# A graph network's first layer: the steps that end a block of 128 nodes moved one pair of edge blocks apart, and the two sort instructions put in separate steps

## The chip, the cores and the metric

The kernel runs on one core of one Trainium2 chip. The metric is the device time of one execution in microseconds. TensorE (PE in the profile) does matrix products and transposes, VectorE (DVE) elementwise work and reductions, ScalarE (ACT) activations and copies, GpSimd (POOL) issues the gathers here, and SyncE (SP) issues most other DMA transfers. [...]

## The reference

Four blocks follow each other on a table x of 6250 nodes by 256 values: a graph layer, a mixture of experts whose gates come from an attention over a second graph, a second graph layer, a second mixture of experts. The change touches the first graph layer. What it computes:

```python
xn = layernorm(x)
row, col = edge_index                       # 106250 edges, sorted by col
h = concatenate([xn[row], edge_attr], axis=1)
h = relu(h @ W1 + b1)                       # 106250 x 256
agg = segment_sum(h, col, num_segments=6250)
cnt = segment_sum(ones, col)
agg = agg / maximum(cnt, 1.0)[:, None]
x = x + relu(concatenate([xn, agg], axis=1) @ W2 + b2)
```

The second block begins with `layernorm(x) @ W_gat` and two dot products per node for the attention; the kernel works these out at the end of each block of 128 nodes of the first layer. Its 131072 edges are sorted by the kernel itself.

## The kernel before

Nodes are kept in 49 blocks of 128, called w in the code. A first stage normalises x and computes the node half of both products: `xn @ W1[0:256] + b1` goes to DRAM (`y_dram`), `xn @ W2[0:256]` stays in SBUF (`b_all`). Then comes the main loop of the layer. For each node block there is a window of 18 x 128 sorted edges, in three groups of six; two blocks of 128 edges are a pair, so a node block takes nine pairs, and the loop runs over 441 pairs k.

What happens to a pair:

- `turn` (line 1367): TensorE transposes the pair's edge attributes (tiles `pt<-ident,ea`, line 1072), ScalarE copies them to SBUF (`et<-pt`, line 1073). It runs three pairs ahead. PSUM holds two such transposed pairs, SBUF four copies.
- `hidden` (line 1382): eight passes of TensorE multiply them by W1 (`ph<-w1b,et`, line 1078), VectorE adds the gathered node half (`yg<-ph,yg`, line 1392), ScalarE applies the ReLU (`h<-yg`, line 1397). It runs one pair ahead. PSUM holds three results `ph`.
- `add_up` (line 1399): once in three pairs, a 0/1 matrix (`eq`, built by VectorE at lines 1163 and 1173) times h adds the group's edges into the node block's sum (`pe<-h,eq`, lines 1410 and 1416). There is one such sum in PSUM.
- `load_sources` (line 1357): once in three pairs GpSimd issues six gathers from `y_dram` (`yg<-y_dram,src`, line 1091) into one of three buffers, and `load_attr` has SyncE load the edge attributes of a later group (line 1290).

Beside the pairs run generators, each advanced by one step per pair: a step is what stands between two `yield`. `end_of(w)` starts one pair after the last group of node block w was added up, and its steps are:

1. VectorE divides the sum by the count (`rc`, `o<-pe,rc`, lines 1425 to 1428) and adds b2 to `b_all` (line 1429).
2. TensorE transposes the quotient (`pt<-ident,o`), ScalarE copies it (`gt<-pt`).
3. TensorE multiplies by the second half of W2 (`pt<-w2b,gt`); VectorE adds, applies the ReLU into x (`o<-pt,b_all`, `x_all`, lines 1437 and 1438) and normalises the new x (lines 1049 to 1062, with one square root on ScalarE, line 1053), which ends in `ln_x`.
4. TensorE transposes `ln_x` (`pt<-ident,ln_x`), ScalarE copies it into `b_all`.
5. TensorE multiplies by W_gat (`pt<-wg,b_all`), ScalarE copies (`hb<-pt`, line 1452), VectorE makes the attention terms (lines 1455 to 1459).
6. After each seventh node block a DMA on ScalarE's queue writes `gat_dram`, from which the next block of the network gathers.

The four TensorE steps share one PSUM pool with two buffers. `background` prepares the next windows (counts at line 969, loads, index arithmetic) and sorts the edges of the second graph: 106 times the eight largest of 1024 keys in each partition (`V.max`, line 1225) and their removal (`V.match_replace`, line 1227).

The program is not laid down in the order of the source. A list scheduler gives each engine its order, with the source order as priority, so that an instruction whose inputs are there can be taken forward. The sort, which depends on nothing in the layer, is taken far forward: it fills VectorE's order up to pair 124 of 441.

Of the kernel before, what the change touches and what calls it, by code (L numbers as in the profile page):

```python
# [841 lines left out]
def kernel(ctx: ExitStack, tc: tile.TileContext, a: dict, out: bass.AP):  # L842
# [62 lines left out]
    with ExitStack() as fast:  # L905
# [60 lines left out]
        def count_below(w):  # L966

            if w:
                V.tensor_scalar(
                    junk, flat, float(w * P), None, op0=OP.is_lt, op1=OP.add,  # L970
                    accum_out=below[:, w : w + 1],
                )

        def count_good():

            V.tensor_scalar(
                junk, flat, N - 0.5, None, op0=OP.is_lt, op1=OP.add,
                accum_out=good[:, NB : NB + 1],
            )
            V.tensor_scalar(  # L980
                junk, flat, -0.5, None, op0=OP.is_lt, op1=OP.add,
                accum_out=good[:, NB + 1 : NB + 2],
            )
            V.tensor_sub(
                good[:, NB : NB + 1], good[:, NB : NB + 1], good[:, NB + 1 : NB + 2]
            )

        def find_starts(pool, b):

            sl = slice(b * TB, (b + 1) * TB)  # L990
            tot = pool.tile([P, D], F32, name="pt")
            TE.matmul(tot[:, 0:TB], ones, below[:, sl], start=True, stop=True)
            V.tensor_scalar(start[:, sl], tot[:, 0:TB], float(E1 - WE), None, op0=OP.min)
# [46 lines left out]
        def nodes(table):  # L1040
            return table[0:NP, :].rearrange("(t p) d -> p t d", p=P)
# [15 lines left out]
        def layer_norm(pool, t0, n):  # L1057

            mv, rs = norm_scale(pool, t0, n)
            xn = pool.tile([P, n, D], F32, name="ln_x", bufs=1)  # L1060
            for i in range(n):
                V.tensor_scalar(
                    xn[:, i, :], x_all[:, t0 + i, :], mv[:, i, 0:1], rs[:, i : i + 1],
                    op0=OP.subtract, op1=OP.mult,
                )
            return xn

        def transposed(psum, dst, src, n=2):

            pt = psum.tile([P, n, P], F32, name="pt")  # L1070
            for c in range(n):
                TE.transpose(pt[:, c, :], src[:, c * P : (c + 1) * P], ident)  # L1072
            SC.activation(dst, pt.rearrange("p c k -> p (c k)"), AF.Copy)  # L1073

        def mm(dst, lhs, rhs, n=2):

            for c in range(n):
                TE.matmul(dst, lhs(c), rhs(c), start=c == 0, stop=c == n - 1)  # L1078
# [140 lines left out]
            )  # L1219
            V.tensor_tensor(key.bitcast(I32)[:, half], raw[0], raw[1], op=OP.bitwise_or)  # L1220

        def sort_step(k):

            top = order[:, k * 8 : (k + 1) * 8]
            V.max(out=top, in_=key)  # L1225
            if k * 8 + 8 < KT:
                V.match_replace(out=key, in_to_replace=top, in_values=key, imm_value=0.0)  # L1227

        def sorted_edges(pst, wk):

            k = order.bitcast(I32)
            V.tensor_scalar(src2, k[:, 0:KA], 8191, None, op0=OP.bitwise_and)
            some = key[:, 0:KT]
            for v, s in ((high, 20), (low, 13)):
                vi = some.bitcast(I32)
                V.tensor_scalar(
                    vi, k, s, 127, op0=OP.logical_shift_right, op1=OP.bitwise_and
                )
                V.tensor_copy(some, vi)
                V.tensor_scalar(some, some, -1.0, 127.0, op0=OP.mult, op1=OP.add)  # L1240
                V.tensor_copy(v, some)
            for c in range(KA // P):
                pt = pst.tile([P, 4, P], F32, name="pt")
                TE.transpose(pt[:, 0, :], some[:, c * P : (c + 1) * P], ident)
                lt = wk.tile([P, P], BF16, name="lt")
                SC.activation(lt, pt[:, 0, :], AF.Copy)
                SC.dma_start(low_dram[c * P : (c + 1) * P, :], lt)
            V.tensor_add(good2[:, 1:2], good3[:, 0, 0:1], good3[:, 1, 0:1])
            V.tensor_add(good2[:, 3:4], good3[:, 0, 1:2], good3[:, 1, 1:2])

            lim = key[:, 0:KA]
            for g in range(KA // G):
                V.memset(lim[:, g * G : (g + 1) * G], float(first_block(g)))
            V.tensor_sub(lim, high[:, 0:KA], lim)
            hit = order[:, 0:KA]
            V.tensor_scalar(hit, lim, 0.0, None, op0=OP.is_ge)
            V.scalar_tensor_tensor(hit, lim, NK - 0.5, hit, op0=OP.is_lt, op1=OP.mult)
            V.tensor_reduce(good2[:, 0:1], hit, axis=AX.X, op=OP.add)
# [5 lines left out]
        with ExitStack() as layer:  # L1264
# [77 lines left out]
            with (  # L1342
# [78 lines left out]
                def end_of(w):  # L1421

                    pe = sums.pop(w)
                    rc = wk.tile([P, 1], F32, name="rc")
                    V.tensor_scalar(rc, pe[:, D:WS], 1.0, None, op0=OP.max)
                    V.reciprocal(rc, rc)
                    ag = wk.tile([P, D], F32, name="o")
                    V.tensor_scalar(ag, pe[:, 0:D], rc, None, op0=OP.mult)
                    V.tensor_add(b_all[:, w, :], b_all[:, w, :], b2)
                    yield  # L1430
                    gt = wk.tile([P, D], F32, name="gt", bufs=1)
                    transposed(psm, gt, ag)
                    yield
                    pm = psm.tile([P, D], F32, name="pt")
                    mm(pm, lambda c: gt[:, c * P : (c + 1) * P], lambda c: w2b[:, c, :])
                    o = wk.tile([P, D], F32, name="o")
                    V.tensor_add(o, pm, b_all[:, w, :])
                    V.scalar_tensor_tensor(
                        x_all[:, w, :], o, 0.0, x_all[:, w, :], op0=OP.max, op1=OP.add
                    )  # L1440
                    xn = layer_norm(wk, w, 1)
                    yield
                    yield
                    transposed(psm, b_all[:, w, :], xn[:, 0, :])
                    yield
                    pg = psm.tile([P, D], F32, name="pt")
                    mm(
                        pg[:, 0:HX], lambda c: b_all[:, w, c * P : (c + 1) * P],
                        lambda c: wg[:, c, :],
                    )  # L1450
                    hb = wk.tile([P, HX], F32, name="hb")
                    SC.activation(hb, pg[:, 0:HX], AF.Copy)
                    pa = wk.tile([P, HX], F32, name="pa")
                    for v, dst in ((att_s, gtab[:, w, HX + H :]), (att_d, a_dst[:, w, :])):
                        V.tensor_mul(pa, hb, v)
                        V.tensor_reduce(
                            dst, pa.rearrange("p (h x) -> p h x", h=H), axis=AX.X, op=OP.add
                        )
                    V.tensor_copy(
                        gtab[:, w, 0:HX].rearrange("p (x h) -> p x h", h=H),  # L1460
                        hb.rearrange("p (h x) -> p x h", h=H),
                    )
                    if w % TB == TB - 1:
                        yield
                        sl = slice(w - TB + 1, w + 1)
                        SC.dma_start(nodes(gat_dram)[:, sl, :], gtab[:, sl, :])

                def background():

                    for b in range(1, NB):  # L1470
                        for w in range(b * TB, (b + 1) * TB):
                            count_below(w)
                            yield
                        find_starts(psm, b)
                        yield
                        load_windows(b)
                        yield
                        if b == 1:
                            count_good()
                            yield  # L1480
                        for k in range((b - 1) * 18, min(b * 18, KT // 8)):
                            sort_step(k)
                            yield
                            yield
                    sorted_edges(psm, wk)

                work = [background()]
                load_sources(0)
                for k in range(3):
# [502 lines left out]
        with (  # L1992
# [253 lines left out]
            k, w, done = 0, 0, 0  # L2246
# [24 lines left out]
        with (  # L2271
# [11 lines left out]
            for i in range(2):  # L2283
                k = NB + 1 + 2 * i
# [52 lines left out]
```

## Time and profile before

| What | us |
|---|---|
| Median of three runs (lowest, highest) | 4402.47 (4393.04, 4404.77) |
| The profiled execution, device time | 4419.4 |
| Its span in the profile | 4417.6 |
| First stage, until the first pair's work, about | 110 |
| Main loop of the first graph layer, about | 110 to 1690 |
| VectorE's sort in it ends at | 596 |
| The rest of the network | 1690 to 4417 |

The span is the time from the first to the last instruction of the one execution that was profiled; times inside it are counted from its start. A row of the profile names the source line, the engine, the operation and the tiles as out<-in, then the count and time; "idle before" is the engine's idle time just ahead of the instruction, and the name after the arrow is what ended it. TensorE's records show when a matmul started; their ends are modelled.

### The profile page before, as it was taken

What the parts mean: (1) busy time and instruction counts of PE and PEld (TensorE: products, weight loads), DVE (VectorE), ACT (ScalarE), POOL (GpSimd) and SP (SyncE); (2) the same over time, 40 slices, a digit from 0 to 9 for tenths busy, and PEclk for the clock granted to TensorE, in tenths of its full rate; (3) what the DMA queues carried; (4) which work ended last, traced back from release to release, by engine and by line L of the source; (5) the groups of instructions that cost most, each with busy time, mean ns of one, the idle gap of its engine ahead of it and who ended that gap; (6) DMA issues with size and microseconds to landing.
All of it is one profiled execution on the core that took longest, in us unless ns stands there. A gap on an engine that the chain in (4) does not pass through costs nothing.

```text
span 4417.6 us, 52878 instructions
## 1 busy us (share of the span) xinstructions
PE 3495.6 (79%) x18190; PEld 2741.9 (62%) x18190; DVE 2195.3 (50%) x5656; ACT 1337.9 (30%) x2703; POOL 2282.5 (52%) x2414
## 2 busy tenths in 40 slices
PE   7889889999998995888889999995156676566677
PEld 3577767777777774777777777873134454444455
DVE  9788853344333342555555565694123343333335
ACT  4333333333333331333333333361011111111113
POOL 0455555555555554455555555003666666666660
PEclk9899999999999997999999999995566666766768
DMA  4445545555454552122222222262111111111110
GB/s 152 125 148 157 147 142 158 148 157 154 148 152 150 161 154 55 45 48 56 47 48 64 49 51 48 77 224 59 44 46 50 48 51 51 51 50 48 54 51 19
DMA packets 270884, 407.13 MB, mean 92 GB/s; under 512 B 116954, under 2 KB 183855, under 8 KB 270608
## 3 DMA queue, kind: packets, MB, share of 16 engines
q1 hardware_dynamic: 171552, 220.55, 16.2%
q0 software_dynamic: 91040, 181.43, 16.0%
q8 instruction: 148, 2.42, 0.2%
q10 hardware_dynamic: 8016, 1.68, 0.2%
q14 instruction: 128, 1.05, 0.1%
HBM read 360.98 MB, written 42.49 MB: 91 GB/s over the span
## 4 chain that ended last, share of the span: by engine, by line
PE 55%; another core or an unknown queue 16%; DVE 12%; issue 9%; ACT 3%; POOL 3%; DMA 1%; SPq 0%; DVEq 0%; ACTq 0%; POOLq 0%
PE ph L1078 24%; PE py L1078 7%; PE pt L1072 6%; PE po L1719 5%; PE pe L2236 3%; PE pt L1078 3%; PE pe L1410 3%; POOL hg L1091 2%; PE pe L1416 2%; DVE eq L2224 1%; DVE x_all L1927 1%; DVE key L1227 1%; DVE yg L1392 1%; DVE order L1225 1%
## 5 line engine op out<-in xcount | busy, mean ns | idle before, releaser
L1091 POOL DMA_INDIRECT yg<-y_dram,src x882 | 841.3, 954 | 817.3 <-issue 235.2
L1091 POOL DMA_INDIRECT hg<-hp_dram,src x882 | 832.3, 944 | 741.6 <-DVE eq L2224 291.1
L1078 PE MATMUL ph<-w1b,et 128*128 128x256 f32 x3528 | 879.6, 390 | 40.9 <-issue 38.9
L1091 POOL DMA_INDIRECT sg<-gat_dram,src x640 | 607.6, 949 | 469.9 <-DVE px L1695 220.0
L1078 PEld LDWEIGHTS ph<-w1b,et 128*128 128x128 f32 x3528 | 653.5, 196 | 130.1 <-issue 56.7
L1392 DVE TENSOR_TENSOR yg<-ph,yg 128x512 f32<-128x512 f32 x441 | 300.4, 687 | 557.3 <-PE ph L1078 228.7
L1078 PE MATMUL py<-w,hh 128*128 128x256 f32 x1568 | 409.5, 393 | 111.4 <-issue 56.1
L2236 PEld LDWEIGHTS pe<-eq,hg 128*128 128x128 f32 x1764 | 337.6, 266 | 211.8 <-DVE eq L2224 95.6
L2236 PE MATMUL pe<-eq,hg 128*128 128x64 f32 (+1 forms) x1764 | 341.2, 350 | 112.3 <-DVE eq L2224 83.5
L1078 PE MATMUL ph<-b_all,w 128*128 128x256 f32 (+1 forms) x1600 | 402.7, 387 | 33.5 <-issue 25.3
L1078 PEld LDWEIGHTS py<-w,hh 128*128 128x128 f32 x1568 | 293.5, 193 | 182.2 <-issue 75.1
L1073 ACT ACTIVATE et<-pt 128x512 f32<-128x512 f32 x441 | 259.2, 593 | 454.4 <-PE pt L1072 305.0
L1078 PEld LDWEIGHTS ph<-b_all,w 128*128 128x128 f32 x1600 | 303.8, 195 | 90.6 <-issue 52.2
L1397 ACT ACTIVATE h<-yg 128x512 f32<-128x512 f32 x441 | 276.7, 629 | 267.9 <-DVE yg L1392 227.7
L2224 DVE TENSOR_SCALAR eq<-px,dst,ew 128x64 f32<-128x64 f32 (+1 forms) x882 | 265.1, 357 | 169.7 <-remote 116.5
L1567 ACT ACTIVATE hh<-ph,b 128x256 f32<-128x256 f32 (+1 forms) x400 | 165.8, 466 | 549.6 <-PE ph L1078 308.7
L1072 PE MATMUL pt<-ident,ea 128*128 128x128 f32 x1764 | 278.9, 279 | 23.5 <-issue 14.7
L1719 PE MATMUL po<-pp,B 128*128 128x240 f32 x1280 | 274.2, 367 | 0.3 <-issue 0.3
L1072 PEld LDWEIGHTS pt<-ident,ea 128*128 128x128 f32 x1764 | 222.9, 146 | 68.9 <-issue 24.3
L1719 PEld LDWEIGHTS po<-pp,B 128*128 128x128 f32 x1280 | 244.3, 191 | 19.1 <-issue 0.5
L1078 PE MATMUL py<-ew,g 65*128 65x256 f32 x392 | 154.6, 521 | 82.0 <-issue 46.2
L1078 PE MATMUL pt<-w2t,gt 128*128 128x256 f32 x98 | 48.1, 585 | 187.7 <-issue 83.3
(301 smaller groups left out, 4445.4 us busy)
## 6 DMA issues: line engine op xcount, KB each, us to landing
ea<-in_edge_attr_dram SPq DMA_DIRECT2D x147, 768.0 KB
y<-y_dram SPq DMA_DIRECT2D x49, 512.0 KB
y_dram<-ys SPq DMA_DIRECT2D x96, 256.0 KB
rb<-low_dram SPq DMA_DIRECT2D x40, 512.0 KB
yg<-y_dram,src POOLq DMA_INDIRECT x882
hg<-hp_dram,src POOLq DMA_INDIRECT x882
sg<-gat_dram,src POOLq DMA_INDIRECT x640
y_dram<-yb SPq DMA_DIRECT2D x49, 128.0 KB
```

Source lines behind the costliest of these rows:

```text
L1072: TE.transpose(pt[:, c, :], src[:, c * P : (c + 1) * P], ident)
L1073: SC.activation(dst, pt.rearrange("p c k -> p (c k)"), AF.Copy)
L1078: TE.matmul(dst, lhs(c), rhs(c), start=c == 0, stop=c == n - 1)
L1091: GP.indirect_dma_start(out=dst, out_offset=None, in_=table[0:NP, :], in_offset=IndirectOffsetOnAxis(ap=idx, axis=0),)
L1392: V.tensor_add(y, ph, y)
L1397: SC.activation(h[:, j : j + 2, 0:D], y, AF.Relu)
L1410: TE.matmul(sums[w][k * HP : (k + 1) * HP, :], eq[:, k * n + j, :], h[:, k * n + j, :], start=g == 0 and j == n - 1, stop=False,)
L1416: TE.matmul(sums[w], eq[:, j, :], h[:, j, :], start=g == 0 and j == G1 - 1, stop=g == NG - 1 and j == 0,)
L1567: SC.activation(hidden[u][:, f, :n, :], ph[:, f - f0, :n, :], AF.Gelu, bias=b1[:, e, f : f + 1],)
L1719: TE.matmul(po.rearrange("p b v -> p (b v)"), B[:, j, :], pp[:, j, :, :].rearrange("p b v -> p (b v)"), start=j == 0, stop=j == G - 1,)
L2224: V.tensor_scalar(equals[k][:, j, to], lanes[:, to], dst1[:, w, g, j : j + 1], ew[:, w, g, j : j + 1], op0=OP.is_equal, op1=OP.mult,)
L2236: TE.matmul(sums[w][:, to], hg[:, j, :], eq[:, j, to], start=g == 1 and j == 0, stop=g == NG - 1 and j == G1 - 1,)
```

## The change

In `end_of`, an empty step is put in after step 1, after step 2, after step 3 (which had one already) and after step 4. So TensorE's transpose of the quotient comes one pair later, the product with W2 two pairs, the transpose of `ln_x` three, the product with W_gat four pairs later than before. The five steps take eleven pairs now, where a node block has nine, so the last one of a block runs beside the first steps of the next. In the sort, the maximum and the removal become two steps of one pair each; before they were one step and an empty step after it.

```diff
-        def sort_step(k):
+        def sort_steps(k):
 
             top = order[:, k * 8 : (k + 1) * 8]
             V.max(out=top, in_=key)
+            yield
             if k * 8 + 8 < KT:
                 V.match_replace(out=key, in_to_replace=top, in_values=key, imm_value=0.0)
+            yield
...
                     V.tensor_scalar(ag, pe[:, 0:D], rc, None, op0=OP.mult)
                     V.tensor_add(b_all[:, w, :], b_all[:, w, :], b2)
                     yield
+                    yield
                     gt = wk.tile([P, D], F32, name="gt", bufs=1)
                     transposed(psm, gt, ag)
+                    yield
                     yield
                     pm = psm.tile([P, D], F32, name="pt")
...
                     xn = layer_norm(wk, w, 1)
                     yield
                     yield
+                    yield
                     transposed(psm, b_all[:, w, :], xn[:, 0, :])
+                    yield
                     yield
                     pg = psm.tile([P, D], F32, name="pt")
...
                         for k in range((b - 1) * 18, min(b * 18, KT // 8)):
-                            sort_step(k)
-                            yield
-                            yield
+                            yield from sort_steps(k)
```

## The prediction

> **What bounds the kernel now.** I read the page first, for the engine that is busy in the first graph layer, then the waits of TensorE in the main loop (110 to 1690 us), then its stretches before and after the end of the sort, and last the timeline of two node blocks. From the page, busy time of each engine and the 40 slices (one is 110.4 us; the layer fills slices 2 to 15):
>
> ```profile
> PE 3495.6 (79%) x18190; PEld 2741.9 (62%) x18190; DVE 2195.3 (50%) x5656; ACT 1337.9 (30%) x2703; POOL 2282.5 (52%) x2414
> PE   7889889999998995888889999995156676566677
> DVE  9788853344333342555555565694123343333335
> PEclk9899999999999997999999999995566666766768
> ```
>
> TensorE is the busiest engine of the layer and never quite full; VectorE is near full only in slices 1 to 5, while it sorts. What TensorE waits for in the main loop, longest total first (us, times, longest):
>
> ```profile
> PE ph L1078 <- issue: 38.9, 53, 2.0
> PE pt L1072 <- DVE ln_x L1062: 33.2, 20, 4.1
> PE pt L1078 <- ACT gt L1073: 20.3, 8, 5.8
> PE pt L1072 <- DVE o L1428: 18.0, 17, 2.3
> PE pt L1072 <- issue: 16.0, 24, 2.2
> PE pt L1072 <- ACT et L1073: 8.5, 10, 3.3
> ```
>
> Three of these six are steps of `end_of`: 33.2 + 20.3 + 18.0 = 71.5 us. That is the most that the spacing can act on directly. The waits on "issue" are not ended by any result that the profile shows. The two halves of the loop, by busy time, granted clock and DMA share:
>
> ```profile
> 110.00:600.00 490.00, 428.39 (x2243) 335.29 (x2242) 409.07 (x802) 174.41 (x371) 255.06 (x267) 0.94 0.49 143
> 600.00:1690.00 1090.00, 996.88 (x5454) 800.82 (x5454) 423.11 (x1099) 409.80 (x877) 586.85 (x618) 0.98 0.51 150
> ```
>
> While it sorts, VectorE is busy for 409 of 490 us (83%); later for 423 of 1090 (39%). GpSimd has time in both. How a step wait comes about, in the timeline of a block at 808 us:
>
> ```profile
> 808.79 0.96 DVE L1173 TENSOR_TENSOR eq<-lane,dst 128x768 f32<-128x768 f32 x1 [3.58 <-PE ph L1078]
> 809.67 0.42 DVE L1437 TENSOR_TENSOR o<-pt,b_all 128x256 f32<-128x256 f32 x1
> ...
> 811.88 0.41 DVE L1062 TENSOR_SCALAR ln_x<-x_all,ln_mv,ln_rs 128x256 f32<-128x256 f32 x1
> 812.35 0.44 PE L1072 MATMUL pt<-ident,ln_x 128*128 128x128 f32 x2 [4.09 <-DVE ln_x L1062]
> 813.06 3.49 PE L1078 MATMUL ph<-w1b,et 128*128 128x256 f32 x8
> ```
>
> VectorE got to `o` late, because its add of a pair came late; the 2.6 us chain to `ln_x` then stood before TensorE for 4.09 us, and the next eight passes took 3.49 us instead of 1.89 at a halved clock. A second kind, at 1075 us:
>
> ```profile
> 1075.37 0.38 PE L1072 MATMUL pt<-ident,o 128*128 128x128 f32 x2
> 1080.51 0.38 ACT L1073 ACTIVATE gt<-pt 128x256 f32<-128x256 f32 x1 [5.20 <-PE pe L1410]
> 1080.94 1.13 PE L1078 MATMUL pt<-w2b,gt 128*128 128x256 f32 x4 [1.58 <-ACT gt L1073]
> 1085.43 0.90 PE L1078 MATMUL ph<-w1b,et 128*128 128x256 f32 x3 [1.74 <-issue]
> ```
>
> Here ScalarE was idle for 5.20 us although the transpose it needs stands 5.1 us earlier: the news of TensorE's work arrived late, and TensorE itself then stood still inside a product. Spacing doesn't remove what causes this.
>
> [...] 0.50 was granted from 813.2 to 816.6 us, after the wait of 4.09. [...] the next copy `et` came at 1082.68, after `gt`. [...]
>
> **The change part by part.** No instruction is added or removed: each engine has the same ones; GpSimd's and SyncE's orders are the same; only TensorE, VectorE and ScalarE are re-ordered within the layer (gathers, attribute loads and window loads stay where they are; the write of `gat_dram` on ScalarE's queue moves with its step). Pace, from the chain of waits: four transposes 0.44 us, eight passes `ph` 1.73, a group's sum 1.45 (half-width) or 2.60.
>
> Count pairs from the one in which the sum is divided. After the sort, TensorE's four steps stood in pairs 3, 4, 6, 7; now in 4, 6, 9, 11. Work of TensorE between them, which is what hides the other engines' part:
> - division to transpose: one pair and a sum more, 0.44 + 1.73 + 1.45 = 3.62 us. The longest wait there is 2.3, so all of it goes but the one at the layer's end. During the sort the step moves by only 1.30 + 1.45 = 2.75, still over 2.3. Of 18.0 I take 15.
> - transpose to W2 product: 0.44 + 1.73 + 1.45 = 3.62 before, two pairs = 4.34 now: 0.72 more (1.6 more during the sort). The waits were 20.3 in 8, up to 5.8, of the second kind. I take 0 to 8, and count 0.
> - W2 product to transpose of `ln_x`: 4.34 before, three pairs and a sum = 7.96 now: 3.62 more against a longest wait of 4.1, and the chain no longer follows the 0.95 us `eq` in the same pair. Of 33.2, 2.8 belong to the last block with nothing to hide it, and about 10 to blocks with the second kind of wait, where TensorE will stand elsewhere. I take 20.
> - W_gat product: waits of nothing today (no row), none later; VectorE's five small instructions (0.17 us each) now stand beside the next block's division, 0.85 us, and that block has 3.62 in hand.
> - the clock: halved stretches of 3.4 or 6.8 us begin at these waits at 417, 543, 813, 844, 1189 us, 20.4 us together, worth 10; I take 7.
> - the sort: 106 maxima of 1.22 and 105 removals of 1.29 us stay, and end at pair 124 as before; per node block VectorE has 12 to 14 of the two both ways. The scheduler had pulled them apart already, mostly one or two per pair. 0, between -5 and +5.
> - buffers: the quotient, `gt` and the PSUM pair of `end_of` are free again before the next block needs them (step five's PSUM is read in pair 11, the next use but one is in pair 15). 0.
>
> Sum 15 + 20 + 7 = 42. During the sort (4.7 of `ln_x`, 12.8 of `o` there) VectorE has only 17% to spare, so part of what TensorE gains there it will meet again as late adds: I take half of some 13 off, 6. At the end the W_gat step of block 47 falls beside block 48's chain: +1. Net -35 to -38; against the span of 4417.6 (device 4419.4) that gives 4382. The profiled execution lies 17 us over the median, so the forecast for the median is 4402.5 - 37 = 4365.
>
> **The rivals.**
> - Waits that only move (a). TensorE can run ahead of VectorE by three `ph` buffers only, and late news of its work delays `yg`, `et` and `gt` alike; then it stands before another instruction for the same time. For: 38.9 + 16.0 us on "issue", which no step explains. Against: at 812 the chain alone was missing. Gain 0 to 12: 4397.
> - Slower (b): ScalarE's queue. `gt` stood behind the ReLU of pair 2; now it stands behind that of pair 4 and ahead of two copies `et`, the first of which TensorE needs 0.44 + 1.73 = 2.17 us after the transpose; `gt` and `et` take 0.38 + 0.60 and a hand-over, so 1.1 us are in hand, where it was 4.3 - 1.1. The view of the tile `gt` after 600 us, idle time before it by what ended it:
>
> ```profile
>   PE pe L1410: 39.6, 8
>   PE ph L1078: 15.2, 5
> ```
>
> These 13 waits have a mean of 4.2 us. If all that is lateness that remains, TensorE loses 13 x (4.2 - 1.1) = 40 us, scaled to 49 blocks 56; less the 37 gained, +19: 4421. It decides once more than about a quarter of the blocks have news over 2.5 us late just there. Against: in these blocks TensorE loses 1.6 + 1.7 + 1.2 already, and can lose them only once.
> - More (c): all 71.5 go but the 4 at the end, with 10 of clock and some of the 8.5 on `et`: -80, 4322. For: neither ScalarE (38% busy after the sort) nor GpSimd is short of time. Against: the "issue" waits.
>
> **How the numbers follow.** Forecast (gain of 13 to 65) 0.57, c 0.13, a 0.14, b 0.16. This kernel's three runs spread by 0.3%, 13 us; less can't be told from none. Of the forecast's 0.57 nearly all is faster; of a, some 0.02 is. Faster 0.71, same 0.13, slower 0.16. The range leaves out the far end of c and most of b: 4318 to 4412. The likeliest case alone spans 4338 to 4390.
>
> **What would show it.** Right: waits of TensorE on `ln_x` fall from 33.2 to under 10 and on `o` from 18.0 to under 4, the loop ends near 1650 instead of 1690, blocks after the sort take about 30.4 us instead of 31.2 (34 divisions lie between 607.4 and 1666.8 us), and everything after is as long as before. Wrong: new waits on `et` or on `yg` of 20 us or more (b, a); "issue" waits grown by what the steps lost (a); a longer first 600 us, with VectorE late by the sort.

## The result, and the profile after

The changed kernel takes 4357.55 us (median of four runs, 4334.86 to 4363.91), the kernel before in the same comparison 4403.62: a ratio of 0.9891, with a 95% interval from 0.9852 to 0.993. The forecast was 4365. The profiled execution took 4357.02 us with a span of 4355.1.

From the page of the changed kernel: busy time, then the slices of TensorE, VectorE and the granted clock.

```profile
PE 3495.9 (80%) x18190; PEld 2755.0 (63%) x18190; DVE 2195.7 (50%) x5656; ACT 1341.3 (31%) x2703; POOL 2298.1 (53%) x2414
...
PE   7899999999999994888889999994156666665667
...
DVE  9798854344333432555555566694123333333335
...
PEclk9899999999999996999999999995566666666668
```

The same work (3495.9 us of TensorE, 3495.6 before) is denser: slices 3 to 15 all read 9 now, where four of them read 8 before. What TensorE waits for in the changed kernel, 110 to 1650 us (us, times, longest):

```profile
PE pt L1072 <- issue: 28.2, 40, 2.2
PE pt L1072 <- DVE ln_x L1062: 26.4, 10, 4.6
PE ph L1078 <- issue: 20.3, 41, 1.6
PE pt L1072 <- ACT et L1073: 12.5, 11, 3.3
...
PE pt L1072 <- DVE yg L1394: 4.4, 3, 2.4
...
PE pt L1078 <- ACT gt L1073: 3.1, 6, 1.0
...
PE pt L1072 <- DVE o L1430: 1.1, 1, 1.1
```

The three step waits are 26.4 + 3.1 + 1.1 = 30.6 us, with the last block. Before, from 110 to 1705 us:

```profile
PE pt L1072 <- DVE ln_x L1062: 36.1, 21, 4.1
PE pt L1078 <- ACT gt L1073: 20.9, 9, 5.8
PE pt L1072 <- DVE o L1428: 19.1, 18, 2.3
```

That is 76.1 us with the last block; the prediction's 71.5 ended at 1690 and missed 4.6 of it. The quotient and `gt` are nearly gone, `ln_x` is not. Issue waits stayed: 28.2 + 20.3 and 8.7 for the product steps make 57.2, where it was 38.9 + 16.0 + 4.9 = 59.8. ScalarE has copied the last product with W_gat at 1646.6 us instead of 1699.6 (-53.0); the rest of the network took 2708.5 instead of 2718.0. Blocks after the sort take 30.14 us instead of 31.16.

The `ln_x` waits that remain all but 2.8 us lie elsewhere than before. The waits of the first 600 us in the changed kernel begin with

```profile
PE pt L1072 <- DVE ln_x L1062: 23.6, 9, 4.6
```

Before, from 110 to 600 us and from 600 to 1640 us:

```profile
PE pt L1072 <- DVE ln_x L1062: 4.7, 4, 1.7
...
PE pt L1072 <- DVE ln_x L1062: 28.6, 16, 4.1
```

In the second stretch the changed kernel has none. So the step is relieved after the sort and worse off during it. The timeline of a block in the sort, changed kernel:

```profile
359.19 0.41 DVE L1441 TENSOR_TENSOR o<-pt,b_all 128x256 f32<-128x256 f32 x1
...
359.52 1.22 DVE L1225 MAX8 order<-key 128x8 f32<-128x1024 f32 x1
...
360.66 0.41 DVE L1442 SCALAR_TENSOR_TENSOR x_all<-o,x_all 128x256 f32<-128x256 f32 x1
360.98 0.68 DVE L1394 TENSOR_TENSOR yg<-ph,yg 128x512 f32<-128x512 f32 x1
...
361.98 1.21 DVE L1228 MATCH_REPLACE8 key<-order,key 128x1024 f32<-128x1024 f32 x1
...
363.70 1.22 DVE L1225 MAX8 order<-key 128x8 f32<-128x1024 f32 x1
...
365.48 0.40 DVE L1062 TENSOR_SCALAR ln_x<-x_all,ln_mv,ln_rs 128x256 f32<-128x256 f32 x1
...
365.94 0.44 PE L1072 MATMUL pt<-ident,ln_x 128*128 128x128 f32 x2 [2.35 <-DVE yg L1394]
```

From `o` to `ln_x` it takes 6.7 us, where it was 2.6 after the sort: three sort instructions, two adds and an `eq` stand in between. (The view puts this wait down to `yg`, but the transpose starts when `ln_x` is there; all of the 4.4 us listed under `yg` stand ahead of this step.) The chain was as long before, though. A block of before in the sort:

```profile
386.37 1.13 PE L1078 MATMUL pt<-w2b,gt 128*128 128x256 f32 x4
388.16 0.41 DVE L1437 TENSOR_TENSOR o<-pt,b_all 128x256 f32<-128x256 f32 x1
395.18 0.40 DVE L1062 TENSOR_SCALAR ln_x<-x_all,ln_mv,ln_rs 128x256 f32<-128x256 f32 x1
395.64 0.44 PE L1072 MATMUL pt<-ident,ln_x 128*128 128x128 f32 x2 [0.19 <-issue]
```

That is 7.4 us, almost without a wait. Over the first 13 blocks `o` to `ln_x` takes 7.1 us in the mean before and 7.5 now. And TensorE's work between the W2 product and this transpose was already that of three pairs before (24 passes of `ph` in each of the 13 blocks, and the whole sum in 8 of them), because the list scheduler had put the transpose that late itself; the change adds almost nothing there. What differs is that VectorE begins `o` 4.1 us after the W2 product starts, not 3.1. So `ln_x` is ready later although it has no more to do. That TensorE, no longer held at the quotient and at `gt`, meets the full VectorE here instead fits these figures; it is a reading, not shown by a run in A.

### The profile page after: what moved, and what is told of

Its sections match the earlier page's. It is cut to its first block, busy times and chain, and to the rows that moved or that the text cites. A ratio compares the mean times of both kernels' runs of the same rounds, so it can differ in the third digit from the quotient of the medians.

```text
span 4355.1 us, 52887 instructions
## 1 busy us (share of the span) xinstructions
PE 3495.9 (80%) x18190; PEld 2755.0 (63%) x18190; DVE 2195.7 (50%) x5656; ACT 1341.3 (31%) x2703; POOL 2298.1 (53%) x2414
## 4 chain that ended last, share of the span: by engine, by line
PE 58%; another core or an unknown queue 15%; DVE 11%; issue 10%; ACT 3%; POOL 1%; DMA 1%; DVEq 0%; ACTq 0%; SPq 0%; POOLq 0%
PE ph L1078 26%; PE py L1078 8%; PE pt L1072 6%; PE po L1723 5%; PE pe L2240 4%; PE pe L1418 3%; PE pe L1412 3%; PE pt L1078 2%; DVE eq L2228 2%; DVE x_all L1931 1%; DVE key L1228 1%; DVE order L1225 1%; POOL yg L1091 1%; ACT hh L1571 1%
## 5 line engine op out<-in xcount | busy, mean ns | idle before, releaser
L1091 POOL DMA_INDIRECT yg<-y_dram,src x882 | 854.1, 968 | 752.0 <-ACT h L1399 305.5
L1078 PE MATMUL ph<-w1b,et 128*128 128x256 f32 x3528 | 879.6, 392 | 21.3 <-issue 20.3
L1078 PE MATMUL py<-ew,g 65*128 65x256 f32 x392 | 156.0, 525 | 64.2 <-issue 26.4
```

What stands on the lines that cost most here:

```text
L1091: GP.indirect_dma_start(out=dst, out_offset=None, in_=table[0:NP, :], in_offset=IndirectOffsetOnAxis(ap=idx, axis=0),)
```

## The experiments

The runs fall into two groups; whether a group goes with the chip or with its condition at the time, they don't separate. Where the recorded comparison and the first four runs were made, the kernel before takes about 4405 us (below: A; 4403.62 and 4408.57). In the other eight runs, on three chips, it takes 3773 us (B: 3773.34, 3773.86 and 3773.19 in three comparisons). Every ratio is to the kernel before on the same chip. A's profiles differ from one another: the profile of the split alone, which is the program of before, ends the layer 19 us earlier (1680.5) than before's did, so that in A only medians over runs settle less than about 20 us.

**The split of the sort alone (A).**

```diff
             V.max(out=top, in_=key)
+            yield
             if k * 8 + 8 < KT:
                 V.match_replace(out=key, in_to_replace=top, in_values=key, imm_value=0.0)
+            yield
```

> Before, with the sort's two instructions in separate steps and nothing else. The order of every engine's instructions comes out the same as before, because the scheduler had pulled them apart already. Spacing theory: 0, so 4402 within 10 us, with the three step waits of TensorE in the loop at 71 +- 15 us; this run also shows how far two profiles of one program differ. Rival (the split carries a part of the gain): 10 us or more below before.

Measured: ratio 0.9996 (0.9979 to 1.0014), step waits 27.5 + 20.9 + 13.7 = 62.1 us. In the profiles every engine has its instructions in the same order as before, so the split does nothing, and what the change does is done by the four empty steps. The 14 us between 62.1 and before's 76.1 are then the spread of one program.

**One empty step alone (A).** Three kernels, each before with one more `yield`: after the first step, after the second, or ahead of the transpose of `ln_x`.

```diff
                     V.tensor_add(b_all[:, w, :], b_all[:, w, :], b2)
                     yield
+                    yield
...
                     transposed(psm, gt, ag)
                     yield
+                    yield
...
                     xn = layer_norm(wk, w, 1)
                     yield
                     yield
+                    yield
```

> Before, with the empty step after step 1 alone: all four TensorE steps come one pair later, and the spacing among them stays as it was. Spacing theory: the waits on the quotient fall from 18 to under 4 us and those on ln_x stay near 33; gt keeps near 20 (its distance is unchanged); the time falls by 10 to 20 us, to about 4387. Rival 1 (the steps stand against each other, one late division delays all): gt falls as well, by some 17, and the time falls by 30 or more. Rival 2 (waits only move): issue waits or ln_x grow by what the quotient lost, time within 8 us of before.

> Before, with the empty step after step 2 alone: the product with the second half of W2 and all that follows it come one pair later. Spacing theory: waits on gt fall from 20 to under 5 us, those on the quotient and on ln_x stay (18 and 33), the time falls by 15 to 20, to about 4385. Rival (gt is waited for because news of TensorE's work comes late, and the time is lost elsewhere all the same): gt falls but et and issue waits grow by as much, time within 8 us of before.

> Before, with the one empty step more ahead of the transpose of ln_x. Spacing theory: after the sort (600 to 1690 us) the waits on ln_x fall from 28.6 to under 5 us, blocks there take 30.5 instead of 31.16 us; during the sort (110 to 600) they stay at some 5, because TensorE is still held at the quotient and at gt there; the time falls by 20 to 30, to about 4378. Rival (VectorE's shortage during the sort is met by whichever step comes last, spacing or not): during the sort ln_x grows to 15 or more in this kernel too.

Measured: first 1.0085 (1.0055 to 1.0115), slower; second 0.9977 (0.9962 to 0.9992); `ln_x` 0.9985 (0.9971 to 1.0). The first was expected to gain and lost, which none of its three expectations had; the second gained 9 us instead of 15 to 20; the third gained 3 instead of 20 to 30. Added up the three are 0.5% slower, where all four steps together make it 1.1% faster. The step after step 4 was not run alone; for the parts to add up it would have to bring 1.6% by itself, ahead of a product for which before shows no wait to speak of (0.5 us in the last block). The first step alone, waits of TensorE from 110 to 1700 us:

```profile
PE pt L1072 <- DVE ln_x L1062: 27.7, 12, 5.7
PE pt L1078 <- ACT gt L1073: 26.5, 8, 4.4
PE pt L1078 <- ACT b_all L1073: 14.1, 6, 4.1
```

The wait of the transpose for the quotient is gone, but `gt` grew and the product with W_gat (which waits for `b_all`) is new. The second step alone, waits from 600 to 1640 us, has W_gat at the top:

```profile
PE pt L1078 <- ACT b_all L1073: 26.7, 10, 4.3
...
PE pt L1072 <- DVE ln_x L1062: 1.7, 2, 1.0
```

A pair isn't a fixed time: in every third pair TensorE also adds up a group, and a step moved by one pair can lose that sum from its cover. The time from start to start of two successive TensorE steps (median after the sort, from the trace; where waits disturb it, the undisturbed blocks) against TensorE's waits from 600 to 1640 us, in A:

| Kernel | transpose to W2; wait for `gt` | W2 to `ln_x`; wait for `ln_x` | `ln_x` to W_gat; wait for `b_all` |
|---|---|---|---|
| before | 3.93; 9.3 | 5.30; 28.6 | 3.93; none listed |
| split alone (the same program) | 3.93; none listed | 5.30; 21.4 | 3.93; none listed |
| first step alone | 2.44; 23.9 | 6.74; 1.0 | 2.44; 14.1 |
| second step alone | 6.15; none | 6.74; 1.7 | 2.44; 26.7 |
| `ln_x` step alone | 3.93; 1.3 | 9.01; none | 2.44; 3.5 |
| all four | 4.61; 1.5 | 8.96; none | 7.15; 0.5 |

With rooms of 4.6 us and more (6.7 for `ln_x`, whose chain is longer) little is left; at 2.44 there are 3.5 to 27 us. The first two rows show how far one program's waits differ, and 2.44 us gives very different waits too, so the room alone doesn't set them; that too little room is the cause is read from this table and was not tested in A by a further run. The first expectation was wrong in saying that the distance to `gt` is unchanged: it shrinks from 3.93 to 2.44. Why a room that the 0.4 us copy needs so little of is too short, shows in the timeline of TensorE in the first-step kernel,

```profile
774.11 0.44 PE L1072 MATMUL pt<-ident,o 128*128 128x128 f32 x2
774.38 0.60 PE L1072 MATMUL pt<-ident,ea 128*128 128x128 f32 x4
774.82 1.81 PE L1078 MATMUL ph<-w1b,et 128*128 128x256 f32 x5
777.67 0.67 PE L1078 MATMUL ph<-w1b,et 128*128 128x256 f32 x2 [1.05 <-issue]
779.08 0.38 PE L1078 MATMUL ph<-w1b,et 128*128 128x256 f32 x1 [0.73 <-issue]
782.32 2.07 PE L1078 MATMUL pt<-w2b,gt 128*128 128x256 f32 x4 [2.86 <-ACT gt L1073]
```

and of ScalarE in the same stretch:

```profile
777.72 0.60 ACT L1073 ACTIVATE et<-pt 128x512 f32<-128x512 f32 x1 [7.38 <-remote]
...
781.27 0.63 ACT L1397 ACTIVATE h<-yg 128x512 f32<-128x512 f32 x1 [2.43 <-DVE yg L1392]
781.80 0.20 ACT L1396 ACTIVATE h<-ones 128x6 f32<-128x6 f32 x1
781.90 0.36 ACT L1073 ACTIVATE gt<-pt 128x256 f32<-128x256 f32 x1
```

The quotient's transpose stands at 774.11, its copy comes at 781.90: ScalarE had stood idle for 7.38 us ("remote" is a release that the profile can't name) although the transposes for that `et` had started at 770.40, and `gt` comes after a ReLU that had waited 2.43 us for a late add. This is the lateness of TensorE's news that the prediction saw at 1075 us. It goes with a loss of clock. From the first division of the layer on, TensorE ran at half clock for 194 us with the first step alone and 151 with the second, against 84 before and 87 with all four (mean granted clock from 110 to 600 and from 600 to 1640 us: 0.91 and 0.94 with the first step alone, 0.94 and 0.98 before); 110 us more at half speed are worth up to 55 (an estimate, half of 110), and the layer is 35 us longer. In the 8 us before a half-clock stretch the longest gap between TensorE's rows is 1.3 us in the mean, in the 39 stretches of the layer with the first step alone as in the 20 of before from the first division on; what makes the clock fall isn't shown.

The `ln_x` step alone fits the rival of waits that only move. Its waits from 600 to 1640 us:

```profile
PE pt L1072 <- issue: 34.4, 50, 1.8
PE ph L1078 <- issue: 27.3, 53, 1.4
PE pe L1410 <- ACT h L1397: 13.9, 15, 1.6
```

The 28.6 us on `ln_x` are gone, as expected. Issue waits rose from 30.2 + 9.8 to 61.7, the sums now wait 13.9 for `h`, and blocks take 31.52 us, not 30.5. During the sort `ln_x` stays at 3.3 (its rival had said 15). TensorE still waits 16.9 us for the quotient there, and its room ahead of the transpose is what before already had, so this says little about the rival.

**One step left out (B).** The changed kernel with one of the four empty steps taken away. Meant to find in A which parts are needed together, they met B.

> The changed kernel without the empty step after step 1 (transposes and products in pairs 3, 5, 8, 10). Theory N (the parts act together: the product with W_gat needs its two pairs of room[...]): waits on the quotient come back, 15 to 25 us, mostly in the sort, and those on ln_x in the sort fall from 28 to some 10, since TensorE is held earlier; ratio to before about 0.993. Theory S (each step by itself, as in the sum): the 15 us of the quotient return, 0.9925. Rival P (the first step alone is harmful, as alone): faster than the changed kernel, 0.985 or less.

> The changed kernel without the empty step after step 2 (pairs 4, 5, 8, 10). Theory N: waits on gt come back, 25 to 35 us as in the first step alone, and with them half-clock time; ratio 0.998 or more. Theory S (the sum counted nothing for gt): 0.989, no difference to the changed kernel.

> The changed kernel without the further empty step before the transpose of ln_x (pairs 4, 6, 8, 10). Theory S: 20 of the ln_x waits return, mainly after the sort, ratio 0.994. Theory N: during the sort TensorE waits for ln_x there more than the changed kernel (28 us to 40), after the sort little (under 10, since two pairs and a sum are still 5.8 us where the chain takes 2.6 and its wait in the first-step run was 4 us in 36 blocks), ratio 0.992.

> The changed kernel without the empty step after step 4 (pairs 4, 6, 9, 10). Theory S (the sum counted nothing for the product with W_gat): 0.989, as the changed kernel. Theory N: TensorE waits 20 to 35 us for the copy into b_all ahead of W_gat, which the first- and second-step runs showed (19 and 34 us), half-clock time in the layer rises from 87 to 130 us or more, ratio 0.999 or more; then this empty step carries as much of the gain as the other three.

Measured: 0.9969 (0.9957 to 0.9981), 0.9956 (0.9942 to 0.9969), 0.9963 (0.9949 to 0.9976), 0.9958 (0.9944 to 0.9971). The numbers expected were A's, so no expectation can be judged by its number. Without the first step TensorE waits 6.3 us for the quotient; in none is `gt` or `b_all` waited for by more than 0.9 us, even where the room is 2.44 (`gt` without the second step). All four reach 27.04 us per block after the sort.

**The four steps without the split (B).** The order of the instructions is that of the changed kernel.

> The four empty steps without the split of the sort; every engine's order comes out as in the changed kernel, so this is also the changed kernel on this call's chip. Two kinds of chip have been met: one where TensorE's results are announced late (before near 4405 us, first two comparisons) and one where they are announced at once (before 3773 us, the four runs that leave one step out). Theory L (the gain depends on how late the news is): 0.989 +- 0.003 where before takes about 4405; 0.9957 +- 0.001 where it takes about 3773, no better than with any one step left out, since those four all reached 27.04 us per block after the sort. Rival (each step adds its own share whatever the chip): 0.989 on both, or at least 0.994 on the second.

**First and fourth step (B).** Before with two empty steps, after step 1 and after step 4.

> Before with the empty steps after step 1 and after step 4 (pairs 4, 5, 7, 9). Late chip, theory N: the waits for W_gat (19 us in the run of the first step alone) go and half-clock time in the layer falls from 194 to 110 us or less, so the ratio turns from 1.0085 to 0.999 or less. Rival (the harm is gt, whose copy comes late and whose wait was 33 us there): waits on gt and half-clock time stay, 1.005 or more. Chip without lateness: no waits on W_gat in either, ratio 0.9965.

**Before once more (B).**

> The kernel before, unchanged, for a profile on this call's chip. Chip without lateness (near 3773 us), theory L: after the sort there is nothing to gain, blocks take 27.04 us as with the four steps, as in the undisturbed blocks of the first profile of before, where no step waits at the old spacing; the whole difference of 15 us lies in the first 13 blocks, as waits on the quotient (10 to 15) and on ln_x. Rival (the spacing gains in every block whatever the chip): after the sort 27.3 us or more per block, 9 us or more of the 15. Late chip (near 4405): another profile of the same program, three step waits 71 +- 15 us and 31 +- 0.5 us per block after the sort.

Measured: 0.9959 (0.9946 to 0.9973), 0.9958 (0.9945 to 0.9972) and 1.0 (0.999 to 1.001). The first two came as expected for a chip without lateness. The rival of the first ("at least 0.994") is met by the number too, but kernels with two, three and four of the steps all take 27.04 or 27.05 us per block after the sort, so the steps don't each add a share there. With the first and fourth step `gt` has only 2.44 us of room and is waited for by 0.5 us. In B the change is worth 15 us, a third of A's 46. In windows of before (columns: busy time of TensorE, its loads, VectorE, ScalarE, GpSimd, then clock, DMA share, GB/s):

```profile
200.00:500.00 300.00, 297.30 (x1697) 243.16 (x1696) 296.49 (x592) 130.39 (x272) 186.71 (x196) 1.00 0.59 172
600.00:1440.00 840.00, 836.95 (x4822) 694.16 (x4821) 372.89 (x959) 379.95 (x778) 527.30 (x556) 1.00 0.59 176
```

and of the four steps alone:

```profile
200.00:500.00 300.00, 297.41 (x1719) 246.91 (x1718) 299.10 (x601) 133.66 (x275) 197.44 (x202) 1.00 0.60 176
600.00:1440.00 840.00, 840.00 (x4859) 700.13 (x4858) 375.09 (x965) 380.30 (x782) 539.21 (x561) 1.00 0.60 177
```

After the sort TensorE is busy for 840.00 of 840 us: nothing is left to hide. But before was at 836.95 already, with three waits on `ln_x`, 3.0 us together; undisturbed blocks fell only from 27.09 to 27.00. Of the 15 us, (27.25 - 27.04) x 34 = 7 lie after the sort and (27.79 - 27.16) x 12 = 8 in it. My expectation that all lies in the sort was wrong by half, and so were its waits on the quotient (3.9 us there, not 10 to 15); the rival, 9 or more after it, doesn't hold either. Most of B's gain isn't waiting that the profile lists: TensorE's idle time in the whole layer fell only from 21.6 to 18.9 us, while the layer is 13.5 us shorter. In the undisturbed blocks the products with W2 and W_gat take 0.2 us less each from start to start, and the transposes of the quotient and of the attributes 0.15 more each; what makes these rows shorter or longer isn't shown. During the sort both engines are nearly full, VectorE for 299.10 of 300 us and TensorE for 297.41; which of them is the bound, the next run asks.

**The sort kept to its pace (B).** The changed kernel, with each sort instruction placed behind the add of its own pair in VectorE's order. The main lines:

```diff
+        def behind(one, at):
+            tc.add_manual_dep(
+                one.ins, at[0].ins.name,
+                mybir.DependencyInfo(mybir.DependencyClass.NoSync, mybir.DependencyReason.DATA),
+                reason="the pace of the sort",
+            )
...
-            V.max(out=top, in_=key)
+            behind(V.max(out=top, in_=key), at)
...
-                    V.tensor_add(y, ph, y)
+                    at[0] = V.tensor_add(y, ph, y)
```

> The changed kernel, with every sort instruction placed behind the add of its own pair in VectorE's order; the scheduler can't take it forward any more, and the sort runs to about pair 244 instead of 124, with at most 9 instead of 12 to 14 sort instructions per block. Theory V (during the sort TensorE waits for ln_x because VectorE is nearly full): late chip, waits on ln_x in the first 13 blocks fall from 28 to under 10 us and the ratio is 0.984; chip without lateness, where some 3 to 5 us of such waits were left, 0.995. Rival (VectorE late in twice as many blocks): waits of 1 to 3 us in blocks 13 to 27, slower than the changed kernel by 10 us or more on the late chip, by 2 or more on the other.

Measured: 0.9944 (0.9931 to 0.9958), 3752.16 us against 3758.79 for the four steps and 3773.86 for before in the same comparison.

```profile
200.00:500.00 300.00, 300.00 (x1736) 250.26 (x1736) 225.12 (x465) 135.59 (x279) 195.07 (x206) 1.00 0.61 180
600.00:1440.00 840.00, 839.99 (x4856) 699.70 (x4855) 482.25 (x1115) 378.62 (x781) 535.78 (x560) 1.00 0.60 176
```

With VectorE at 225 instead of 299 of 300 us, TensorE is busy throughout in the sort as well, blocks there take 26.81 us (27.16), and the blocks after it pay nothing (27.05 us) although the sort reaches into them, to 939 us. The slowest of its five runs (3753.84) is below the fastest of the four steps' (3755.26). That VectorE was short in the sort is thereby shown in B. It is the best of these kernels there; in A it wasn't tried.

## Why the prediction was right, and where its sum was not

The forecast of -37 us met -46, and the loop end (1650; 1646.6), the block time (30.4; 30.14), the unchanged rest and the issue waits that didn't grow came as said. One of its own signs of being right did not: `ln_x` was to fall under 10 us and stands at 26.4. The terms, in A, changed kernel against before, and in brackets against the split alone, which is the same program as before:

- Quotient, 15: 19.1 - 1.1 = 18.0 recovered (19.8). Right.
- `gt`, 0 (0 to 8): 20.9 - 3.1 = 17.8 recovered (10.6), outside its bounds either way. The room was counted rightly (0.72 more; 0.68 measured), but taking these waits for the second kind, which spacing doesn't remove, was wrong: with all four steps the lateness is still there (a third of TensorE's announcements after the sort over 1 us late), and TensorE pays little for it at `gt`. Why 0.7 us more should be enough isn't shown.
- `ln_x`, 20, less 6 for VectorE: 36.1 - 26.4 = 9.7 recovered (1.1), which is 28.6 gained after the sort and 18.9 lost in it. That TensorE would meet again part of what it gains in the sort was right, but it was sized at 6, a third of what came, and placed on late adds, where it was `ln_x`. The sum also took 4.34 us of room before for the whole layer; in the sort there were 6.5 to 8.0 us of work there already (an estimate from the rows' number and the pace), so the step had next to nothing to win. The 2.8 us of the last block stayed, as said, but weren't in the 33.2.
- W_gat, 0: TensorE's idle time at its rows rose from 0.9 to 10.6 us over 49 blocks, 8.5 of it between the parts of a product, which the waits view counts among those on issue. It has 7.15 us of room and waits 0.9 us for its copy, so the copy isn't what is missing; what ends these stops isn't shown.
- Clock, +7: nothing. Half-clock time from the first division on was 84 us before and 87 after. The trace of before has 0.50 granted after the wait of 4.09 us; that such waits make the clock fall was the author's estimate, and no run shows it.
- Sort split, 0: shown by its own run.
- Rivals: slower by ScalarE's queue (b) didn't come, `gt` and `et` together fell from 29.4 to 15.6. "Waits only move" (a) fits the `ln_x` step alone, not all four.

All waits in the ten largest rows together fell from 153.9 to 110.3 us, by 44, of which 45.5 are the three steps'; the loop is shorter by 53, and the other 9 are within what two profiles of one program differ by there. So the forecast was right in direction, and that its size came so near is in part luck, since errors offset each other: `gt` too small by 11 to 18, `ln_x` with its VectorE term too large by 4 to 13, the clock by 7. What the sum could not show is that it isn't a sum: each term was taken as the effect of one step's own move, and by themselves three of these moves change the time by -0.2% to +0.9%. Open is which of the four steps A needs together, since the runs that leave one out met B; the table of rooms speaks for all rooms at 4.6 us or more, but no kernel between was run there.

## What to carry to other kernels

Work out the room of a step as time on the engine that waits, between the two neighbouring steps and with everything that stands there now and then (here a sum in every third pair), and do so for the steps behind the moved one as well: moving one alone can take another's cover away (here the room to `gt` fell from 3.93 to 2.44 us). Before adding distance, look at which engine is full in that stage; where VectorE is at 99% (299.10 of 300 us in B's sort), pace the work that fills it instead (blocks there then took 26.81 us, not 27.16). And ask how much of a gain depends on where the kernel runs: it was 46 us where results were announced late and 15 where they were not.

## What the runs showed of the hardware

The same program, before, took about 4405 us in A and 3773 in B, 14% less (profiled span 3770.0 instead of 4417.6; the first layer ends at 1492.1 instead of 1699.6). The view of the tile `gt` after 600 us, before in B, idle time of ScalarE before it by what ended it:

```profile
  PE pt L1072: 29.2, 33
```

That is 0.88 us each of 33, always ended by its own transpose; in A eight of them had 39.6 us. By the trace's semaphore events, about a third of TensorE's announcements after the sort (30 to 34%, each instruction matched with the next update) came over 1 us behind the modelled end of their instruction in the six profiles of A, and none in those of B. Before spent 84 us of the layer, from its first division on, at half clock in A and 5 in B; TensorE's idle time in the layer was 159.6 us in A and 21.6 in B. What delays the announcements, and whether it belongs to the chip or to its condition at the time, no run here shows.
